# 951 no-operations on TensorE, 45 regroupings and 9 loads on ScalarE's queue, and another order, in a cross attention with layer normalisation

## The chip, the cores and the metric

The kernel runs on one core of one Trainium2 chip. The engines of a core are TensorE (PE; its weight loads are listed as PEld), VectorE (DVE), ScalarE (ACT), GpSimd (POOL) and SyncE (SP). SP computes nothing here; it issues DMAs, and ACT and POOL can issue them too, from the same stream that holds their computing instructions. The metric is the time of one execution in microseconds on the device. Before the change it is 519.78 us, the median of 3 runs (518.49 to 520.38).

## The reference, cut to what matters

```python
def ref(q, k, v, wq, wk, wv, wo, gamma, beta, mask):      # q: (4, 2048, 512), k = v: (4, 77, 512)
    qs = (q @ wq) in 16 heads of 32; ks_, vs = k @ wk, v @ wv in 16 heads of 32
    scores = einsum('bhqd,bhkd->bhqk', qs, ks_) / sqrt(32)
    scores = where(mask, -inf, scores)
    attn = einsum('bhqk,bhkd->bhqd', softmax(scores), vs)  # back to (4, 2048, 512)
    out = attn @ wo + q
    return (out - mean(out)) / sqrt(var(out) + 1e-5) * gamma + beta
```

8192 rows of queries, 77 keys in each of 4 batches, everything in float32. A float32 product of the two large projections is made as three products of rounded parts (high by high, low by high, high by low).

## The kernel before, in words

The 8192 rows are 64 tiles of 128; two tiles are a block, four a group. Each word of a long table, ORDER, is one step: a letter and the number of a group, tile or block. The program reads the table from left to right and each engine gets its instructions in that order; nothing else schedules. A second table, SLOTS, says which buffer each tile takes. Semaphore waits are added where one engine needs what another made, and where a buffer is overwritten.

- `g` loads a half group of the transposed x (xtf, line 262), `i` casts it to its high part (xth, ACT), `j` makes the low part (xtl, POOL). `Q` is a visit of TensorE to one of a group's four query projections: 12 matmuls of 128x512 into one bank (pq, line 275); `q` copies it out (DVE).
- `S` makes the scores of one tile: 32 matmuls in the program, which the chip runs as 64 with a weight load each (sc, line 405). `T` adds the mask and takes the maxima, a quarter of the heads at a time (DVE, line 422), `e` is the exponentials with their sums (ACT, line 437), `r` the reciprocals (DVE), `n` the normalising (POOL, line 452), `t` transposes 32x32 pieces of the tile into the block's buffer B (DVE, line 473).
- `P` with block, part and queue is one regrouping DMA (line 484): a block takes 12 of them, B to PT, which puts the keys on the partitions. The last block has `U`, the same by tile. The last letter names the issuing queue: s for SP, a for ACT, g for POOL. B and PT have two buffers each.
- `V` is the product with the values, 16 heads of one block (pa, line 498), `a` and `b` split it into a high part AH (ACT) and a low part AL (DVE), `O` is a visit to the output projection of one tile, 12 matmuls (po, line 554). `x` loads the residual rows (line 539), `+` adds them (DVE), `s` takes the moments, `v` the reciprocal square root (POOL), `k` scales (ACT), `f` and `)` apply gamma and beta (POOL), `w` stores (SP, line 601).

A queue handles its steps in order: a regrouping on SP that waits for its transposition holds the loads and stores behind it, and one on ACT or POOL holds that engine's computing instructions behind it. A block's `V` comes three blocks after its scores, so each engine works on other tiles at one time. Where the values' product follows a score tile, `early_waits` puts the product's DMA waits ahead of that tile.

Of the kernel before, what the change touches and what calls it, by code (L numbers as in the profile page):

```python
# [8 lines left out]
F32 = mybir.dt.float32  # L9
# [4 lines left out]
ALU = mybir.AluOpType  # L14
# [3 lines left out]
P = 128  # L18
# [16 lines left out]
for b in range(4):  # L35
# [15 lines left out]
T1.1 Q4 T1.2 e0.3 F0 T1.3 I0 e1.2 r0 n0 S2 q4 e1.0 S3 T2.3 T2.0 Q7 N Y0 x1 Q5 i5 F1 e1.1 F3 R2 e1.3 j5 i4 t0 T2.2 r1  # L51
F2 n1 e2.2 g6 T3.3 T3.0 T3.2 T2.1 j4 t1 P0.3s P0.2s P0.0s P0.5s e3.3 Q6 q6 G0 q7 B0 B2 e2.0 G3 G1 D0 e2.1 q5 e3.2 T3.1
P0.9s e2.3 r2 e3.1 e3.0 i6 G2 g7 P0.10s P0.11s S4 T4.3 e4.3 P0.7s T4.2 P0.8s i7 e4.2 B1 r3 Z1.s T4.0 e4.0 n2 T4.1 t2
Z0.s Q10 P0.4s n3 t3 P0.6s D2 P0.1s Z3.s S6 T6.2 T6.0 j6 D1 T6.3 P1.3s q10 T6.1 e4.1 r4 P1.0s P1.5s Q9 q9 e6.0 S5 T5.2
T5.0 e6.1 P1.2s P1.1s P1.8s j7 Q14 Z16.s P1.6s n4 t4 S7 Z2.s T7.3 e5.2 e6.3 e6.2 e7.3 T7.0 e7.0 T7.2 T5.3 T5.1 r6
P1.11s T7.1 e7.1 e7.2 q14 P1.10s P1.9s P1.7s P1.4s Q8 q8 Q11 q11 r7 Q13 n6 t6 e5.3 e5.1 e5.0 S9 T9.0 n7 T9.3 t7 r5 n5
V1 a1.0 T9.1 T9.2 a1.1 e9.0 b1.1 b1.0 t5 Z11.s x3 g8 g9 Z5.s Z13.s V0 a0.0 a0.1 P3.9s P3.3s Q12 S8 q13 T8.0 T8.2 e9.1
P3.4s P3.5s e9.3 b0.0 T8.3 O3 S10 i8 b0.1 L1 e8.0 T10.0 x5 P2.9s +3 e9.2 P3.2s P2.3s r9 O2 T8.1 q12 P3.8s e8.3 j8
P2.5s x2 Z4.s P3.1s O1 P2.4s P3.7s s3 O0 P3.6s =24.8 T10.1 +2 P3.10s e8.2 e8.1 P3.0s P3.11s s2 Z12.s x0 T10.3 n9 Q15
r8 v1 e10.1 i9 P2.6s e10.3 g11 +1 P2.1s T10.2 P2.0s n8 P2.10s Y1 e10.0 t9 P2.11s +0 e10.2 k3 t8 Z6.s q15 S11 k2 j9  # L60
T11.2 T11.1 r10 x7 V3 S12 T11.0 Q17 Z15.s T12.1 P4.2s T11.3 s0 =16.8 s1 P4.4s i11 Q18 n10 Q16 e11.1 q17 a3.0 a3.1
P2.8s P2.7s T12.3 b3.1 f3 T12.2 )3 T12.0 e11.0 v0 P2.2s Z14.s b3.0 e11.2 t10 e11.3 P4.7s P4.6s S13 g10 q18 P4.9s j11
# [7 lines left out]
T18.2 b5.0 n16 +8 +9 T18.3 P6.1s t16 Q22 S19 V6 e17.3 q23 q22 P7.3s f5 P7.11s P7.7s x11 T19.1 P7.2s e17.1 T19.0 T19.2  # L70
r17 P7.0s i15 P7.5s e18.3 n17 w1 s9 a6.0 i14 e18.0 P7.9s P7.4s S20 O10 b6.0 j15 t17 a6.1 T19.3 s8 P7.6s T20.2 Q24
e18.2 Q27 r18 )4 T20.1 T20.3 x10 e19.2 e19.0 e19.3 e19.1 )6 +10 T20.0 S21 b6.1 P7.10s n18 )5 q27 q24 O12 e20.3 P7.8s
w4 g16 O11 s10 P8.11s e20.1 w6 e20.2 r19 n19 e20.0 x12 P8.9s t18 T21.1 T21.2 V7 v4 e21.2 j14 f7 T21.3 t19 P8.10s +12
S22 T21.0 r20 O13 P8.8s P8.6s P8.0s k8 )7 e21.1 k9 T22.1 Q26 T22.3 +11 a7.0 P8.2s P8.4s P8.1s T22.0 Q25 P9.9s P9.10s
# [21 lines left out]
n34 e36.0 e36.1 e35.0 P16.11s s27 )23 P16.2s O28 O29 P16.10s T36.3 t34 S37 P16.5s T36.2 +28 s28 f24 +29 r35 P16.7s
P16.0s e36.3 T37.1 T37.3 V15 j22 x32 n35 T37.2 w25 e36.2 g25 e37.1 e37.2 a15.1 S38 T37.0 a15.0 j23 t35 P17.9s r36
P17.2s n36 s29 T38.3 e37.0 s26 b15.0 T38.0 P17.5s Q42 T38.1 e37.3 P16.3s b15.1 Q41 Q43 q41 P16.8s v14 q42 T38.2 Q40
S39 )24 v13 t36 q43 q40 e38.3 k28 e38.0 r37 T39.3 x30 g24 V16 P17.4s e38.1 T39.2 e38.2 =56.8 k27 r38 P17.7s T39.1 n37
w23 P17.8s T39.0 t37 S40 P17.10s P17.3s i24 a16.0 a16.1 T40.0 i25 e39.1 T40.1 e39.2 P17.6s O30 j24 e39.3 n38 e39.0 k26  # L100
f27 T40.2 P17.1s j25 b16.0 f28 O31 b16.1 x31 P17.11s P17.0s O32 +30 s30 T40.3 e40.0 t38 g26 e40.1 e40.3 r39 S41 w24
P18.1s e40.2 +32 P18.2s +31 P18.9s n39 )28 T41.3 P18.4s P18.11s V17 T41.1 S42 k29 e41.3 T41.0 t39 r40 Q44 T42.3 Q45
)27 T42.2 P18.7s P18.8s e41.1 n40 f29 T42.1 a17.1 P18.6s P18.5s x33 O33 T41.2 q44 T42.0 P19.11s a17.0 P18.3s P19.0s
b17.0 b17.1 s31 e41.0 Q46 P18.0s P19.10s P19.4s P19.1s e42.2 w27 P18.10s P19.9s P19.7s e41.2 v15 e42.0 q45 r41 +33 )29
e42.3 V18 P19.3s s32 e42.1 s33 x34 t40 P19.5s q46 r42 a18.1 S43 Q47 k30 n41 w29 g27 T43.3 v16 k33 a18.0 e43.3 P19.8s
t41 i27 k31 T43.2 O34 P19.2s P19.6s T43.1 T43.0 b18.0 q47 f30 f33 S44 e43.1 n42 j27 f31 )31 t42 O35 w28 T44.3 T44.2
T44.1 P20.6s P20.9s f26 e43.0 +34 e43.2 P20.3s k32 S45 T44.0 V19 x35 P20.10s g28 i26 b18.1 O37 r43 n43 e44.3 )33 T45.1
# [67 lines left out]
def xattn_layernorm(  # L175
# [625 lines left out]
```

## Time and profile before

| what | us |
|---|---|
| median of 3 runs | 519.78 |
| the profiled execution | 521.82 |
| its span, first to last instruction | 519.9 |
| PE busy | 502.0 (97%) |
| ACT busy | 474.9 (91%) |
| DVE busy | 459.8 (88%) |
| POOL busy | 420.6 (81%) |
| mean granted clock of TensorE | 0.995 |

Busy time counts an engine as busy while an instruction of its own is in it. TensorE's matmuls overlap each other in the records (one is listed with 0.39 us and the next starts 0.23 later), so its busy share says little about holes; a timeline shows them in brackets, with what ended them. "issue" is said where the engine waited for nothing that the profile shows. SPq, ACTq and DVEq are the sequencers of those engines, which issue DMAs and handle waits. By kind, the DMAs before the change are 396 regroupings (344 issued by SP, 21 by ACT, 31 by POOL), 64 loads of residual rows, 64 stores and the loads of the transposed x, of weights and masks.

### The profile page before, as it was taken

How to read it: one execution, taken by the hardware profiler on the slowest of the kernel's cores; microseconds unless marked ns; L12 is line 12 of the kernel's file. 1: busy time of each engine (PE TensorE's matmuls, PEld its weight loads, DVE VectorE, ACT ScalarE, POOL GpSimd, SP SyncE). 2: the span in 40 equal slices, each digit the busy share in tenths (PEclk: the TensorE clock that was granted, in tenths of full speed). 3: DMA queues.
4: the chain of work that ended last, by engine and by line, in shares of the span. 5: the costliest groups of instructions: out<-in, count | busy, mean ns of one | idle time of the engine just before them, and what ended most of it. 6: DMA issues, size and time to landing. Idle time of an engine off the chain costs nothing.

```text
span 519.9 us, 20339 instructions
## 1 busy us (share of the span) xinstructions
PE 502.0 (97%) x6831; PEld 386.9 (74%) x6831; DVE 459.8 (88%) x2539; ACT 474.9 (91%) x2248; POOL 420.6 (81%) x387
## 2 busy tenths in 40 slices
PE   9999999999999998999999999999999998999895
PEld 7987778776677776777687777778777776877664
DVE  6799998998979897899898999897989988999987
ACT  6699999998999998799989999999998798899872
POOL 3566447886858999698789979799998989899986
PEclk9999999999999998999999999999999999999999
DMA  8947667889867786688877797867795859878657
GB/s 309 395 173 174 146 178 191 217 211 212 249 179 194 186 258 174 193 223 240 223 217 195 200 244 195 233 196 201 225 264 153 240 163 224 229 216 214 170 156 270
DMA packets 58782, 110.86 MB, mean 213 GB/s; under 512 B 9462, under 2 KB 11278, under 8 KB 58678
## 3 DMA queue, kind: packets, MB, share of 16 engines
q1 hardware_dynamic: 54502, 101.30, 69.0%
q0 software_dynamic: 2496, 5.77, 4.1%
q10 hardware_dynamic: 1680, 2.49, 1.9%
q8 instruction: 54, 0.88, 0.8%
q14 instruction: 50, 0.41, 0.3%
HBM read 41.79 MB, written 16.78 MB: 113 GB/s over the span
## 4 chain that ended last, share of the span: by engine, by line
PE 62%; POOL 10%; ACT 7%; DMA 7%; SPq 5%; DVE 4%; issue 3%; DVEq 0%; ACTq 0%; POOLq 0%
PE pq L275 25%; PE po L554 19%; PE sc L405 8%; PE pa L498 7%; ACT pbuf L437 5%; POOL pbuf L452 4%; DMA PT<-B 4%; SPq L484 3%; DVE B L473 2%; POOL o L598 2%; PE pv L326 2%; POOL PT L484 1%; PE pk L299 1%; PE pq L685 1%; ACT o L592 1%
## 5 line engine op out<-in xcount | busy, mean ns | idle before, releaser
L437 ACT ACTIVATE pbuf<-pbuf,nm 128x77 f32<-128x77 f32 x1024 | 352.3, 350 | 13.2 <-DVE nm L422 9.0
L437 ACT ACTIVATION_READ_ACCUMULATOR pbuf<-pbuf,nm 128x1 f32 x1024 | 195.0, 190 | 0.0
L452 POOL TENSOR_TENSOR pbuf<-pbuf,ri 128x1232 f32<-128x1232 f32 x63 | 142.3, 2259 | 50.6 <-DVE ri L447 37.3
L422 DVE CUSTOM_DVE_ANT_0 pbuf<-sc,mb 128x77 f32<-128x77 f32 x1024 | 170.2, 231 | 7.9 <-PE sc L405 5.4
L473 DVE STREAM_TRANSPOSE B<-pbuf 128x1280 f32<-128x1280 f32 x64 | 96.1, 1503 | 16.6 <-POOL pbuf L452 7.5
L554 PE MATMUL po<-woh,AH 128*128 128x512 f32 x256 | 103.8, 405 | 0.0
L554 PE MATMUL po<-wol,AH 128*128 128x512 f32 x256 | 100.6, 393 | 0.0
L554 PE MATMUL po<-woh,AL 128*128 128x512 f32 x256 | 100.5, 393 | 0.0
L275 PE MATMUL pq<-xth,wqh 128*128 128x512 f32 (+1 forms) x256 | 99.9, 390 | 0.2
L275 PE MATMUL pq<-xtl,wqh 128*128 128x512 f32 (+1 forms) x256 | 98.2, 383 | 0.0
L275 PE MATMUL pq<-xth,wql 128*128 128x512 f32 (+1 forms) x256 | 98.1, 383 | 0.0
L422 DVE DVE_READ_ACCUMULATOR2_ANT nm<- 128x1 f32 x1024 | 83.7, 82 | 0.0
L405 PEld LDWEIGHTS sc<-kct,q 32*64 32x64 f32 x4096 | 52.8, 130 | 31.9 <-issue 19.9
L595 POOL TENSOR_TENSOR o<-o,gam 128x512 f32<-128x512 f32 x56 | 72.0, 1291 | 2.3 <-ACT o L592 2.1
L598 POOL TENSOR_TENSOR o<-o,bet 128x512 f32<-128x512 f32 x56 | 71.8, 1290 | 1.1
L269 POOL TENSOR_TENSOR xtl<-xtf,xth 128x1024 fp32r<-128x1024 f32 x28 | 67.1, 2400 | 6.9 <-ACT xth L265 6.2
L405 PE MATMUL sc<-kct,q 32*64 32x77 f32 x4096 | 63.6, 238 | 7.7 <-issue 3.7
L498 PE MATMUL pa<-PT,vsb 96*32 96x256 f32 x992 | 59.8, 382 | 2.7 <-DMA xtl<-x 2.0
L554 PEld LDWEIGHTS po<-woh,AH 128*128 128x128 f32 x256 | 48.3, 189 | 14.3 <-issue 1.1
L275 PEld LDWEIGHTS pq<-xth,wqh 128*128 128x128 f32 x256 | 48.2, 188 | 11.4 <-issue 0.8
L554 PEld LDWEIGHTS po<-woh,AL 128*128 128x128 f32 x256 | 48.5, 189 | 10.6
L275 PEld LDWEIGHTS pq<-xth,wql 128*128 128x128 f32 x256 | 48.1, 188 | 9.6
(108 smaller groups left out, 638.7 us busy)
## 6 DMA issues: line engine op xcount, KB each, us to landing
PT<-B SPq DMA_DIRECT2D x330, 128.0 KB
xtf<-xT SPq DMA_DIRECT2D x28, 512.0 KB
o<-x SPq DMA_DIRECT2D x56, 256.0 KB
out<-o SPq DMA_DIRECT2D x56, 256.0 KB
PT<-B POOLq DMA_DIRECT2D x25, 128.0 KB, 4.6
PT<-B ACTq DMA_DIRECT2D x17, 128.0 KB
stage_a<-kin SPq DMA_DIRECT2D x4, 410.0 KB
xtf<-xT SPq DMA_DIRECT2D x4, 256.0 KB
```

Of the source, the lines that this page charges most:

```text
L269: return nc.gpsimd.tensor_tensor(l[:, c : c + 2], fx.pop((g, c)), xh[g][:, c : c + 2].bitcast(F32), ALU.subtract)
L275: nc.tensor.matmul(pq, w[:, c, m * P : (m + 1) * P], r[g][:, c, rs], start=(n == 0), stop=(n == 11))
L405: mm = nc.tensor.matmul(sc[j][r0 : r0 + SR, g * NK : (g + 1) * NK], qs[q, g, rs.start + r0 : rs.start + r0 + SR], kct[q, g, t // TPB, keys ...
L422: nc.vector.tensor_tensor_reduce(pb[:, h // 2, (h % 2) * NK : (h % 2 + 1) * NK], scs[t][j][:, g * NK : (g + 1) * NK], mb[:, t % TPB, keys_ ...
L437: nc.scalar.activation(pb[:, h // 2, (h % 2) * NK : (h % 2 + 1) * NK], pb[:, h // 2, (h % 2) * NK : (h % 2 + 1) * NK], AF.Exp, bias=nmax[t ...
L452: return nc.gpsimd.tensor_tensor(pv, pv, rv.to_broadcast((P, NP, 2, NK)), ALU.mult)
L473: nc.vector.transpose(bt.rearrange("p c q r -> p q c r"), pbuf[t % NPB].rearrange("p q (c r) -> p q c r", c=5),)
L484: parts.setdefault(b, []).append(queue.dma_start(pt[32 * c : 32 * c + 32, i, :, cols], src))
L498: nc.tensor.matmul(pas[b, g // 2][HD * j : HD * (j + 1), (g % 2) * BLK : (g % 2 + 1) * BLK], vsb[:, 2 * b // TPB, h % 2, HD * (h // 2) : H ...
L554: nc.tensor.matmul(pos[t], a[:, c, rs], w[:, c, :], start=(first and c == 0 and n == 0), stop=(c == NC_D - 1 and n == 2),)
L595: return nc.gpsimd.tensor_tensor(od[t], od[t], gam, ALU.mult)
L598: return nc.gpsimd.tensor_tensor(od[t], od[t], bet, ALU.add)
```

## The change: what it does

Every step of ORDER is still there once, so each engine computes the same operations with the same shapes. Four things differ.

1. `Q` and `O` may carry a number after a dot: so many no-operations are spread among the 12 matmuls of the visit, at most 24, two behind each matmul. 951 are in the program, in visits from group 1's query projection (Q4.16) to group 14's, and one in the output projection of tile 57.
2. The queue letters of 82 regroupings differ. 39 go from SP to ACT, 14 from ACT to SP, 21 from POOL to SP, 5 from SP to POOL and 3 from POOL to ACT. ACT then issues 49 (45 for blocks and 4 for the last block's tiles), POOL 12, SP 335. Before, ACT's and POOL's stood in blocks 23 to 31; now ACT's stand in most blocks from 3 on.
3. `x` may carry a 1: ACT issues that load. These are the loads of tiles 13, 14, 27, 46, 52, 56, 58, 60 and 63. (`g` and `q` have such a switch too, which no word uses, and so has `k`, so the sets CENTRED and IN_PSUM are empty.)
4. The order of the words differs from the 200th word on, and with it some buffers in SLOTS.

```diff
-T1.1 Q4 T1.2 e0.3 F0 T1.3 I0 e1.2 r0 n0 S2 q4 e1.0 S3 T2.3 T2.0 Q7 N Y0 x1 Q5 i5 F1 e1.1 F3 R2 e1.3 j5 i4 t0 T2.2 r1
+T1.1 Q4.16 T1.2 e0.3 F0 T1.3 I0 e1.2 r0 n0 S2 q4 e1.0 S3 T2.3 T2.0 Q7.24 N Y0 x1 Q5.21 i5 F1 e1.1 F3 R2 e1.3 j5 i4 t0
...
-    def q_rows(pq, m, g, rs):
+    def pad(n, nops):
+        for _ in range((n + 1) * nops // 12 - n * nops // 12):
+            nc.tensor.nop(hint="pad")
+
+    def q_rows(pq, m, g, rs, nops=0):
...
                 nc.tensor.matmul(pq, w[:, c, m * P : (m + 1) * P], r[g][:, c, rs], start=(n == 0), stop=(n == 11))
+                pad(n, nops)
                 n += 1
...
-    def load_x(t):
+    def load_x(t, by_scalar):
...
-        nc.sync.dma_start(od[t], x[t * P : (t + 1) * P, :])
+        (nc.scalar if by_scalar else nc.sync).dma_start(od[t], x[t * P : (t + 1) * P, :])
...
-    def o_proj(t):
+    def o_proj(t, nops=0):
...
                     stop=(c == NC_D - 1 and n == 2),
                 )
+                pad(3 * c + n, nops)
...
-        "Q": lambda k, part: q_visit(*divmod(k, 4)), "q": lambda k, part: q_evac(*divmod(k, 4)),
+        "Q": lambda k, part: q_visit(*divmod(k, 4), part), "q": lambda k, part: q_evac(*divmod(k, 4), part),
...
-        "x": lambda k, part: load_x(k), "X": lambda k, part: resid(k), "O": lambda k, part: o_proj(k),
+        "x": lambda k, part: load_x(k, part), "X": lambda k, part: resid(k), "O": lambda k, part: o_proj(k, part),
```

TensorE behind the scores of tile 26, the place of the longest hole in its timeline before. Names carry a number of their own at the end; sc is a bank of scores, po one of the output projection. Before:

```order
1585 L405 MATMUL sc_2_3557<-kct,q_2919 64x77
1586 L405 MATMUL sc_3_3558<-kct,q_2919 64x77
1587 L554 MATMUL po_3614<-woh,AH_3374 128x512
1588 L554 MATMUL po_3614<-wol,AH_3374 128x512
1589 L554 MATMUL po_3614<-woh,AL_3394 128x512
```

and now:

```order
1811 L414 MATMUL sc_2_3948<-kct,q_3220 64x77
1812 L414 MATMUL sc_3_3949<-kct,q_3220 64x77
1813 L563 MATMUL po_4013<-woh,AH_3653 128x512
1814 L276 NO_OP x2
1815 L563 MATMUL po_4013<-wol,AH_3653 128x512
1816 L276 NO_OP x2
1817 L563 MATMUL po_4013<-woh,AL_3749 128x512
1818 L276 NO_OP x2
```

The output projection that follows these scores carries 24 no-operations, and 226 rows more stand ahead of it than before.

SP's queue at the regroupings of blocks 13 and 14 before (PT_14 is block 14's; o_22 a load of residual rows):

```order
176 L262 DMA xtf_10_0_4376<-xT 128x1024
177 L484 DMA PT_14_4380<-B_14_4327 32x2x512 x2
178 L484 DMA PT_13_4169<-B_13_3991 32x2x512
179 L539 DMA o_22_4394<-x 128x512
180 L484 DMA PT_13_4169<-B_13_3991 32x2x512
181 L484 DMA PT_14_4380<-B_14_4327 32x2x512
182 L539 DMA o_23_4434<-x 128x512
183 L484 DMA PT_13_4169<-B_13_3991 32x2x512 x2
184 L484 DMA PT_14_4380<-B_14_4327 32x2x512 x2
```

Now three of block 14's are on ACT, between exponentials, scalings of o and casts of AH:

```order
186 L536 CAST AH_12_4925<-pa_12_0_4854 128x512
187 L493 DMA PT_14_4954<-B_14_4820 32x2x512
188 L609 ACTIVATE o_21_4573<-o_21_4573,rn_10_4877 128x512
189 L609 ACTIVATE o_19_4334<-o_19_4334,rn_9_4822 128x512
190 L536 CAST AH_12_4925<-pa_12_1_4855 128x512
191 L446 ACTIVATE pbuf1_81,sum_31_4846<-pbuf1_81,nm_31_4827 128x77 x8
192 L493 DMA PT_14_4954<-B_14_4820 32x2x512
```

POOL behind the normalising of tile 53 before, with regroupings of block 26 among its products with gamma and beta:

```order
285 L452 TENSOR_TENSOR pbuf2_82<-pbuf2_82,ri_53_7530 128x8x154
286 L595 TENSOR_TENSOR o_44_7263<-o_44_7263,gam_76 128x512
287 L484 DMA PT_26_7702<-B_26_7528 32x2x512 x3
288 L595 TENSOR_TENSOR o_45_7341<-o_45_7341,gam_76 128x512
289 L598 TENSOR_TENSOR o_44_7263<-o_44_7263,bet_77 128x512
290 L484 DMA PT_26_7702<-B_26_7528 32x2x512
291 L452 TENSOR_TENSOR pbuf0_80<-pbuf0_80,ri_54_7704 128x8x154
```

and now, without them:

```order
285 L461 TENSOR_TENSOR pbuf2_82<-pbuf2_82,ri_53_8503 128x8x154
286 L272 TENSOR_TENSOR xtl_15_8357<-xtf_15_2_7888,xth_15_8161 128x1024
287 L612 TENSOR_TENSOR o_45_8086<-o_45_8086,gam_76 128x512
288 L612 TENSOR_TENSOR o_44_8224<-o_44_8224,gam_76 128x512
289 L615 TENSOR_TENSOR o_45_8086<-o_45_8086,bet_77 128x512
290 L461 TENSOR_TENSOR pbuf0_80<-pbuf0_80,ri_54_8696 128x8x154
```

Block 26 had seven regroupings on POOL and ACT; now it has two, on ACT.

More of the change, by code (lines that the diff above doesn't have):

```diff
@@ L70 @@
[L70 to L74, printed above, removed]
@@ L96 @@
[L96 to L100, printed above, removed]
@@ L101 @@
[L101 to L105, printed above, removed]
@@ new lines @@
+T42.1 T42.2 k31 Q45.8 i24 Q46 P19.4s e42.3 q45 P19.3s q47 T42.0 r40 a17.1 e42.1 e42.0 v16 =48.8 q44 V18 b17.1 n41 g26
+)26 n40 f31 t41 a18.0 P19.7a P19.9s t40 q46 S43 T43.1 w29 k32 P19.11s b18.0 O34 T43.0 +34 T43.2 a18.1 T43.3 k30 P20.0s
+O35.11 P20.10a e42.2 r42 x35 P20.7s S44 T44.1 j24 b18.1 T44.3 f32 )31 P20.11s T44.0 P19.8s f27 P19.10a Q48.24 +35
+T44.2 e43.1 e43.2 )27 w31 P19.1s n42 )32 i26 P19.5s w27 e43.0 t42 S45 O36.24 x36 P20.2s g27 k33 s34 e44.3 x37 e43.3
+T45.2 Q51.24 w26 P20.3a V19 j26 q48 f30 e44.1 T45.3 r43 e44.2 P20.6a P20.4s P20.8s P20.1s +36 g29 T45.0 P20.5s e44.0
@@ new lines @@
+n43 f33 q51 i27 e45.3 P20.9s )33 a19.0 e45.0 w32 s36 T45.1 )30 t43 P21.10s s35 P21.11a e45.1 r44 S46 a19.1 P21.8g
+T46.1 e45.2 n44 e46.1 x40 O37.17 P21.1s v17 b19.0 +37 T46.2 j27 P21.5s T46.3 T46.0 Q50 P21.2s Q49.24 P21.9s P21.7s r45
+e46.2 e46.0 t44 k34 b19.1 n45 S47 q50 q49 k35 f35 T47.1 V20 T47.2 P21.3s e46.3 T47.0 s37 P21.0s v18 i29 g28 f34 e47.0
+t45 S48 a20.0 O39.24 k36 T48.2 b20.0 T48.0 w30 )34 x39 w33 r46 +39 T47.3 T48.3 P22.6s x38 a20.1 e47.2 k37 O38.22 Q55.2
+i28 n46 T48.1 b20.1 P21.4s P22.2s +38 S49 O40.13 =56.8 e47.1 f36 w34 f37 e47.3 x42 P21.6s s38 e48.0 O41.15 e48.2
@@ L142 @@
+U63.3g b30.1 ~57 U62.0s U63.6g U63.8g y56 k54 u56 &58 O61 O60 y59 s58 U62.8a W62 y57 f55 k53 u58 U63.2s &61 u57 ~61
+)55 U63.0s w52 z56 w48 z59 c62 y58 &60 w51 z57 W63 y61 X63 d62 w59 w55 w56 z58 u61 ~60 f53 c63 z61 w49 w61 y60 d63 O62
+w57 u60 f54 )54 )53 z60 w54 w60 w58 w53 &62 s62 u62 O63 y62 s63 z62 y63 u63 w62 z63 w63
 """
 ALONE = {int(w[1:]) for w in ORDER.split() if w[0] in "u@"}
+CENTRED = {int(w[1:].split(".")[0]) for w in ORDER.split() if w[0] == "k" and "." in w}
+IN_PSUM = {int(w[1:].split(".")[0]) for w in ORDER.split() if w[0] == "k" and w.endswith(".2")}
@@ L739, in xattn_layernorm @@
             ins = ops[op](int(k or 0), int(part or 0))
-            if op in "FG":
+            if op in "FG" or op == "k" and k and int(k) in CENTRED - IN_PSUM:
                 shared = ins
-            elif shared and op in "jnf)":
-                wait_for(ins, shared, "VectorE's pass over two tiles of SBUF is begun ahead of GpSimd's")
+            elif shared and op in "jnf)v":
+                wait_for(ins, shared, "VectorE's pass over both of its ports is begun ahead of GpSimd's")
                 shared = None
```

207 lines of the change are left out of this document (109 added, 98 removed).

## The prediction

> **What bounds the kernel now.** I read the page's busy line first, then the chain of waits in order of time, then TensorE's timeline where that chain leaves it, and last the queues' own waits.
>
> ```profile
> PE 502.0 (97%) x6831; PEld 386.9 (74%) x6831; DVE 459.8 (88%) x2539; ACT 474.9 (91%) x2248; POOL 420.6 (81%) x387
> 126.41 2.72 PE po L554 x12
> 132.73 1.86 PE pa L498 x32
> 139.83 2.97 PE po L554 x12
> 148.23 0.88 PE sc L405 x52
> ```
>
> The rows of the chain are start, length, what. TensorE's visits have fixed lengths: a projection visit (pq or po, 12 matmuls) 2.72 us, or 2.97 between two visits of another shape; a score tile (sc) 0.88, a values product (pa) 1.86. With 64 po, 60 pq, 64 sc and 32 pa visits that is 174 + 163 + 56 + 60 = 453 us of a span of 519.9, and the rest is the start (the first 21 us), the changes of shape and the holes. So TensorE sets the time wherever it is not waiting, and what can be won is the sum of its holes. The timeline of TensorE shows them in brackets:
>
> ```profile
> 119.03 0.94 PE L405 MATMUL sc<-kct,q 32*64 32x77 f32 x64 [0.85 <-DMA PT<-B]
> 122.53 0.73 PE L405 MATMUL sc<-kct,q 32*64 32x77 f32 x40 [0.23 <-DVE nm L422]
> 138.81 1.02 PE L405 MATMUL sc<-kct,q 32*64 32x77 f32 x60 [0.97 <-issue]
> 151.99 0.35 PE L405 MATMUL sc<-kct,q 32*64 32x77 f32 x4 [0.16 <-issue]
> 199.53 0.29 PE L405 MATMUL sc<-kct,q 32*64 32x77 f32 x2 [2.59 <-issue]
> 254.60 1.05 PE L405 MATMUL sc<-kct,q 32*64 32x77 f32 x64 [0.39 <-DMA out<-o]
> 258.12 0.31 PE L405 MATMUL sc<-kct,q 32*64 32x77 f32 x2 [0.33 <-DVE nm L422]
> 258.75 0.89 PE L405 MATMUL sc<-kct,q 32*64 32x77 f32 x58 [0.32 <-DVE nm L422]
> 438.60 0.94 PE L405 MATMUL sc<-kct,q 32*64 32x77 f32 x64 [1.53 <-DMA PT<-B]
> 442.08 0.89 PE L405 MATMUL sc<-kct,q 32*64 32x77 f32 x58 [0.32 <-DVE nm L422]
> 482.09 1.93 PE L498 MATMUL pa<-PT,vsb 96*32 96x256 f32 x32 [0.78 <-DMA out<-o]
> 494.41 1.94 PE L498 MATMUL pa<-PT,vsb 96*32 96x256 f32 x32 [1.97 <-DMA xtl<-x]
> 507.01 1.08 PE L513 MATMUL pa<-PT,vsb 96*32 96x128 f32 x32 [0.21 <-DMA out<-o]
> ```
>
> Three holes have the releaser "issue" and stand in the middle of a score tile: 0.97 + 0.16 + 2.59 = 3.72 us. Seven follow a regrouping or VectorE's maxima: 0.85 + 0.23 + 0.39 + 0.33 + 0.32 + 1.53 + 0.32 = 3.97. Three are in the last 40 us: 0.78 + 1.97 + 0.21 = 2.96. Together 10.65 us.
>
> **The no-operations (the "issue" holes).** No tile is late at these three holes, so the instruction itself was. The page's queue list and a count between the holes say why:
>
> ```profile
> q8 instruction: 54, 0.88, 0.8%
> 138.83:151.99 13.16, 13.00 (x253) 10.02 (x252) 11.47 (x68) 13.16 (x63) 5.98 (x5) 1.00 0.80 236
> 151.99:199.53 47.54, 44.95 (x626) 34.40 (x627) 41.39 (x234) 47.54 (x237) 44.16 (x36) 1.00 0.70 193
> ```
>
> The stage rows count TensorE's matmuls and weight loads: 253 + 252 between the first two holes, 626 + 627 between the second and the third. With the 9 and 27 semaphore waits that the built program has there (and an edge of one or two), this is 512 and 1280, that is 2 and 5 times 256; and 54 instruction packets for 13,662 matmuls and loads are one for each 253. TensorE's instructions come in blocks of 256, and each of these holes is the first instruction of a block. Counted on from there, the shortest block of the kernel before (a score tile, a values product, most of a second score tile) is consumed in 3.2 us, and the hole at 199.53 shows a block that came later than its use. In the changed order, counting each no-operation as one instruction, I summed by the visit lengths above the work between a block's predecessor's start and its own, with the issue allowed half a score tile (64 instructions) of lead, an assumption: the smallest such time is 3.6 us before and 7.1 us after, and 2 blocks were under 4 us before, none after. So 951 no-operations move the block edges out of the dense stretches. The last hole costs more than itself:
>
> ```profile
> 196.94 2.59 issue
> 199.82 4.54 PE po L554 x12
> 200.00:250.00 50.00, 50.00 (x643) 38.70 (x643) 45.22 (x258) 44.91 (x212) 42.49 (x39) 0.97 0.78 217
> ```
>
> The visit behind it took 4.54 instead of 2.97, with a granted clock of 0.97 in that stage: 1.6 us. All of it is 3.72 + 1.6 = 5.3 us; bounds 0 and -5.3. I take **-4.7**, nearly all, since every margin at least doubles where it was tight. The Trainium skill (Runtime: NRT & Kernel Launch, Instruction fetch mechanics) gives blocks of 256 instructions, as the count does, but calls the crossing "mostly hidden"; the trace has 2.59 us for one, so the trace decides; by the page this term would be 0 and the sum 4.7 us higher.
>
> Their own price: the trace has no no-operation, so I go to the nearest rows, instructions that only the sequencer handles.
>
> ```profile
> 254.26 0.05 DVEq L473
> 254.31 0.05 issue
> 254.36 0.05 DVEq L473
> ```
>
> One wait and the gap behind it are 0.10 us. A visit carries at most 24 no-operations, 2.4 us; its 24 loads and matmuls are issued at no more than 0.88 / 128 = 0.007 us each (a score tile issues 128), 0.17 us. 2.57 is under the 2.72 for which the array is busy, so that visit hides them. If the cover is gone, because a wait had emptied TensorE's queue, the following score tile starts without lead; the row at 138.81 shows 1.02 us for a tile that starts so, against 0.88. Bounds 0 and 25 such tiles at 0.14, +3.5; I take **+1.0**, nearer to 0, as such waits are few.
>
> **The regroupings and loads.** A block of two tiles is regrouped by 12 DMAs, 344 of the 396 issues on SP. The chain and the queue's waits:
>
> ```profile
> SPq L484 <- DVE B L473: 77.7, 25, 7.4
> 242.73 1.44 DVE B L473
> 250.40 1.24 SPq L484
> 251.68 2.54 DMA PT<-B
> 113.10 5.84 DMA PT<-B
> ```
>
> From the end of a transposition (242.73 + 1.44 = 244.17) to the issue that the next one waits for (250.40 + 1.24 = 251.64) pass 7.5 us in which SP issues one DMA after the other, regroupings of blocks 13 and 14 and x loads between them; the transfer itself takes 2.5. The next transposition must wait, since it overwrites the same B buffer, and behind it on VectorE stand maxima that the score tiles' banks wait for: the holes at 254.60 to 258.75. The one at 119.03 ends the same way behind a transfer of 5.84. The change puts 3 of block 14's regroupings and one of block 13's on ScalarE, one more of 13 on GpSimd, and x loads of tiles 13, 14, 27, 46, 52, 56, 58, 60 and 63 on ScalarE. Three issues fewer at 0.6 us are 1.9 us off that chain, more than any of these holes but the sum at 438 to 442 (1.85). Bounds 0 and -4.0; I take **-3.5**, since 39 regroupings leave SP for ScalarE in blocks 3 to 30. The Trainium skill (DMA: Bandwidth & Descriptors, Issuing engines are not separate DMA queues) says issuing from several engines saves only the sequencer's time, "usually small relative to the DMA itself". Here 7.5 us of issue stand against 2.5 of transfer, so the trace disagrees; by the page this term would be near 0.
>
> From block 23 on the other direction rules: GpSimd issues 12 regroupings in all instead of 31, and 14 of ScalarE's go to SP.
>
> ```profile
> L484 POOL DMA_DIRECT2D PT<-B x31 | 17.3, 562 | 3.8 <-issue 1.3 <-DVE nm L422 1.0 <-DMA out<-o 0.7
> 350.00:480.00 130.00, 128.15 (x1831) 98.27 (x1833) 117.01 (x670) 119.98 (x586) 119.39 (x121) 1.00 0.77 211
> ```
>
> 19 at 0.56 are 10.7 us given back to GpSimd, which is busy for 119.39 of 130 us there and carries the normalising that the last blocks wait for; SP had room. The tail's three holes (2.96) shrink by what GpSimd no longer issues ahead of the last products, 1 to 2 issues: **-1.0**, bounds +1 and -3.
>
> What ScalarE pays: 58 issues instead of 21, 37 more. Two rows of it:
>
> ```profile
> 408.29 0.59 ACTq L484 DMA_DIRECT2D PT<-B  x1
> 408.93 0.36 ACT L437 ACTIVATE pbuf<-pbuf,nm 128x77 f32<-128x77 f32 x1 [2.71 <-DVE nm L422]
> 409.15 0.59 ACTq L484 DMA_DIRECT2D PT<-B  x1
> 409.20 0.19 ACT L437 ACTIVATION_READ_ACCUMULATOR pbuf<-pbuf,nm 128x1 f32 x1
> 100.00:350.00 250.00, 244.17 (x3427) 187.17 (x3426) 223.56 (x1299) 241.27 (x1155) 212.71 (x176) 0.99 0.78 212
> ```
>
> The second issue lies under exponentials that were already queued and costs nothing; the first came into an idle engine and, if that idle had ended sooner, would cost 0.59. If all 37 were bare it is 22 us of ScalarE, which has 250 - 241.27 = 8.7 us of idle in the middle stretch; if all are covered, 0. The new ones stand among runs of exponentials, like the second. What waits behind one, at block 14: two scalings, the cast of AH of block 12 and then exponentials. I take **+0.9**: a few bare ones, mostly in ScalarE's own idle time.
>
> **The order.** Engines' operations are the same in number and shape. TensorE enters and leaves its projections 47 and 46 times instead of 49 and 48; a pair of such changes is 2.97 - 2.72 = 0.25: **-0.5**.
>
> **Sum.** -4.7 + 1.0 - 3.5 - 1.0 + 0.9 - 0.5 = -7.8. The profiled execution took 521.82 us (span 519.9 and 1.9 around it), so 514.0 by its own measure; the median of the runs shown, 519.78, is 2.04 below it, so **512.0** against that median.
>
> **Rivals.** (1) The block edges fall elsewhere than I count, or the blocks come late through the load on the DMA engines (0.70 to 0.80 share in the rows above) whatever the margin: then only the no-operations' price stays of that part, -7.8 + 4.7 = -3.1, 516.7. For it speaks the hole at 138.81, whose block is not among the shortest; against it, all three holes stand exactly on the edges. Its chance is 0.18. (2) The holes only move: ScalarE (91%) and VectorE (88%) have little more room than TensorE, and a tile that is scored sooner waits for its exponentials; 519.8, chance 0.12. (3) Slower: an issue on ScalarE waits for a transposition and all exponentials stand behind it. SP waited for one in 25 of its regroupings, 77.7 us, 3.1 each, 7% of 344. If ScalarE meets the same at its 49 regroupings, 49 x 0.07 x 3.1 = 11 us are lost, more than -7.8 wins: 523. It decides from some 10 us of such waits on. Against it: before, the ScalarE group of exponentials waits only 1.8 us in all for a regrouping:
>
> ```profile
> L437 ACT ACTIVATE pbuf<-pbuf,nm 128x77 f32<-128x77 f32 x1024 | 352.3, 350 | 13.2 <-DVE nm L422 9.0 <-DMA PT<-B 1.8 <-POOL pbuf L464 1.2
> ```
>
> Chance 0.10.
>
> **How the numbers follow.** The forecast has 0.60, the rivals 0.18, 0.12 and 0.10. Faster by over 0.5% means below 517.2, slower above 522.4; half a per cent is what a measurement of this kernel can tell from no change. The forecast nearly always and three quarters of rival 1 are faster: 0.59 + 0.14 = 0.73. Same: the rest of these and most of rival 2, 0.17; slower 0.10. All holes of TensorE gone (10.65) with the slow visit (1.6) and the changes of shape (0.5) give 521.82 - 12.75 - 2.04 = 507.0; the waits also stretch visits that show no hole, some 3 us (the visit before 119.03 among them), so the low end is 504.0. The high end, 519.5, takes in rival 1 and the nearer half of rival 2.
>
> **What would show it.** Right: no hole of "issue" inside a score tile, no stage with a clock under 1.00 before the tail, 57 or 58 instruction packets on q8, SP's wait for B well under 77.7, and score tiles at 0.88 behind padded visits. Wrong: score tiles of 1.0 us and more behind padded visits (the no-operations are not hidden), "issue" holes as before (rival 1), exponentials that wait for a transposition with a ScalarE issue ahead of them (rival 3), or the same 10 us of holes at other places (rival 2).

## The result, and the profile after

| | before | changed |
|---|---|---|
| median, us | 519.71 (516.25 to 525.76, 20 runs) | 516.66 (512.36 to 525.17, 20 runs) |
| ratio | | 0.9936, 95% interval 0.9911 to 0.9961 |

The change makes the kernel faster by 0.64%, some 3.3 us. That is the direction that was forecast and inside its range, but 7.8 us were expected: less than half came. The timed executions of one kernel spread over 9 us and more here, so small differences are read from the ratios and their intervals, and a single profile shows where a wait is and not how much time it is worth. The ratios leave out executions that took over 1.5% more than the fastest of their kernel; by the two medians alone it would be 0.9941. The profile of the changed kernel shown here is from a second run of the same code (ratio 0.9946, see the first experiment); its profiled execution took 515.81 us, its span 514.0. The execution profiled first took 521.18 us.

The busy line of the changed kernel, and its queue of instruction packets:

```profile
PE 500.9 (97%) x6831; PEld 385.9 (75%) x6831; DVE 457.7 (89%) x2539; ACT 474.0 (92%) x2248; POOL 410.8 (80%) x368
q8 instruction: 58, 0.95, 0.8%
```

TensorE still sets the time, with the same busy time less 1.1 us. The 58 packets are those of a program that is longer by 951 instructions. TensorE's timeline, all holes over 0.15 us behind the start (in brackets the hole and what ended it):

```profile
135.24 0.47 PE L282 MATMUL pq<-xth,wql 128*128 128x512 f32 x1 [0.59 <-issue]
250.97 0.90 PE L414 MATMUL sc<-kct,q 32*64 32x77 f32 x58 [0.23 <-DVE nm L431]
298.99 0.56 PE L414 MATMUL sc<-kct,q 32*64 32x77 f32 x34 [0.50 <-issue]
358.08 1.07 PE L507 MATMUL pa<-PT,vsb 96*32 96x256 f32 x16 [0.71 <-DVE AL L540]
360.00 0.31 PE L414 MATMUL sc<-kct,q 32*64 32x77 f32 x2 [0.38 <-DVE nm L431]
360.64 0.89 PE L414 MATMUL sc<-kct,q 32*64 32x77 f32 x58 [0.32 <-DVE nm L431]
406.38 0.31 PE L414 MATMUL sc<-kct,q 32*64 32x77 f32 x2 [0.38 <-DVE nm L431]
406.92 0.90 PE L414 MATMUL sc<-kct,q 32*64 32x77 f32 x58 [0.23 <-DVE nm L431]
437.36 0.89 PE L414 MATMUL sc<-kct,q 32*64 32x77 f32 x58 [0.32 <-DVE nm L431]
452.76 0.34 PE L414 MATMUL sc<-kct,q 32*64 32x77 f32 x2 [0.16 <-DVE q L298]
453.38 0.90 PE L414 MATMUL sc<-kct,q 32*64 32x77 f32 x58 [0.28 <-DVE nm L431]
477.56 1.93 PE L507 MATMUL pa<-PT,vsb 96*32 96x256 f32 x32 [0.95 <-DVE o L575]
```

Together they are 5.05 us where the kernel before had 10.65. "issue" is 1.09 of it (3.72 before), and no hole is longer than 0.95 (2.59 before). No hole ends with a regrouping here; those that end with VectorE's maxima (nm) remain, at other places.

The execution profiled first is less clean. Its holes over 0.15 us are 8.07 us in all, one of them behind a regrouping (0.37), and its two of "issue" are 2.48:

```profile
135.88 0.47 PE L282 MATMUL pq<-xth,wql 128*128 128x512 f32 x1 [1.61 <-issue]
442.59 0.52 PE L414 MATMUL sc<-kct,q 32*64 32x77 f32 x30 [0.87 <-issue]
```

So the signs that the prediction named came in part: 58 packets and score tiles at 0.88 came, but each profile has a hole of "issue" inside a score tile, and the first one has a stage (from 250 us) at a clock of 0.97.

### The profile page after: what moved, and what is told of

It reads as the page before. It is cut to its first block, busy times and chain, and to the rows that moved or that the text cites. A ratio compares the mean times of both kernels' runs of the same rounds, so it can differ in the third digit from the quotient of the medians.

```text
span 519.4 us, 21286 instructions
## 1 busy us (share of the span) xinstructions
PE 503.4 (97%) x6831; PEld 387.5 (75%) x6831; DVE 459.0 (88%) x2539; ACT 474.6 (91%) x2248; POOL 411.2 (79%) x368
## 4 chain that ended last, share of the span: by engine, by line
PE 48%; POOL 12%; DMA 11%; ACT 9%; DVE 9%; SPq 5%; issue 5%; ACTq 0%; DVEq 0%; POOLq 0%
PE pq L282 18%; PE po L563 16%; ACT pbuf L446 7%; PE sc L414 6%; PE pa L507 5%; DMA PT<-B 5%; SPq L493 4%; POOL pbuf L461 4%; DVE pbuf L431 3%; POOL o L615 2%; DVE B L482 2%; POOL xtl L272 2%; DMA o<-x 2%; POOL o L612 2%; DMA out<-o 2%
## 5 line engine op out<-in xcount | busy, mean ns | idle before, releaser
L446 ACT ACTIVATE pbuf<-pbuf,nm 128x77 f32<-128x77 f32 x1024 | 355.9, 383 | 15.3 <-DMA o<-x 6.1
L446 ACT ACTIVATION_READ_ACCUMULATOR pbuf<-pbuf,nm 128x1 f32 x1024 | 228.8, 223 | 0.0
L414 PEld LDWEIGHTS sc<-kct,q 32*64 32x64 f32 x4096 | 54.0, 130 | 29.9 <-issue 14.9
L414 PE MATMUL sc<-kct,q 32*64 32x77 f32 x4096 | 65.6, 238 | 4.7 <-DVE nm L431 3.2
L563 PEld LDWEIGHTS po<-woh,AL 128*128 128x128 f32 x256 | 48.1, 188 | 10.5
```

The source lines that it names most:

```text
L414: mm = nc.tensor.matmul(sc[j][r0 : r0 + SR, g * NK : (g + 1) * NK], qs[q, g, rs.start + r0 : rs.start + r0 + SR], kct[q, g, t // TPB, keys ...
L446: nc.scalar.activation(pb[:, h // 2, (h % 2) * NK : (h % 2 + 1) * NK], pb[:, h // 2, (h % 2) * NK : (h % 2 + 1) * NK], AF.Exp, bias=nmax[t ...
L563: nc.tensor.matmul(pos[t], a[:, c, rs], w[:, c, :], start=(first and c == 0 and n == 0), stop=(c == NC_D - 1 and n == 2),)
```

## The experiments

In all of them "changed" is the changed kernel and "before" the kernel before; every ratio is against the kernel before, timed on the same chip. One per cent is 5.2 us.

### The parts, taken away from the changed kernel

**The same code again** (no edit).

> The changed kernel once more, timed against the kernel before on one chip, so that the other runs of this set have it beside them. Expected 0.9936 of before within 0.3%, some 516.5 us. Theory A (the no-operations removed most of the instruction holes, and the moved regroupings only moved the other holes): the profile again has at most one or two holes of issue, and waits for VectorE's maxima at several score tiles that together are 8 to 13 us of stretched visits. Theory B (all parts gave a little): holes of both kinds are shorter than before.

0.9946 [0.9908, 0.9984], median 516.63.

**Without the no-operations:**

```diff
-Q4.16 ... Q7.24 ... Q5.21 ...
+Q4 ... Q7 ... Q5 ...          (all 951 taken away)
```

> The changed order, queues and loads, without the 951 no-operations. Edges of blocks of 256 instructions fall again where they fall; five blocks hold less than 5 us of TensorE's work counted from 33 instructions ahead of the block before, against none with the no-operations. Theory A: 2 to 5 us longer than the changed kernel, near 520, with 2 to 5 holes of issue inside score tiles, some with a visit at a lower clock behind them. Rival (the no-operations neither help nor cost): within 1 us of the changed kernel, 516.5. Rival (they cost sequencer time): 1 to 3 us shorter, 514.

1.0012 [0.9974, 1.0050], median 521.87. TensorE's waits of this kernel (us in total, times, longest):

```profile
PE sc L414 <- issue: 3.5, 2, 2.4
PE pa L507 <- DMA PT<-B: 2.7, 1, 2.7
PE pa L507 <- DVE AL L540: 1.9, 1, 1.9
```

and of the changed kernel, those of "issue":

```profile
PE pq L282 <- issue: 0.6, 1, 0.6
PE sc L414 <- issue: 0.5, 1, 0.5
```

The no-operations are worth 1.0012 - 0.9946 = 0.66%, 3.4 us (the two intervals, taken together, leave 0.6 to 6.2), and without them the kernel is as fast as the one before. Everything else in the change is thus worth +0.6 us, between -1.4 and +2.6, where the forecast had -4.1.

**All block edges moved by 61 instructions**, by leaving 61 of the 951 out near the start:

```diff
-Q4.16 ... Q7.24 ... Q5.21
+Q4 ... Q7 ... Q5
```

> The changed kernel with the first three padded visits (Q4, Q7, Q5 of group 1) bare: 61 no-operations fewer, 890 left at the same places. Every later edge of a block of 256 moves by 61 instructions, into the dense stretches: 9 blocks then hold less than 5 us of work, 6 of them 3.4. Theory A (what counts is where the edges fall): longer than the kernel without any no-operations or equal to it, 520 to 525, with 4 or more holes of issue. Rival (what counts is that no-operations slow TensorE's issue): within 1 us of the changed kernel, 516.5.

1.0243 [1.0194, 1.0292], median 533.1: 3% slower than the changed kernel, with 890 of its 951 no-operations and the same work in the same order, and slower than the 520 to 525 us that were expected. Its waits and its chain at the first hole:

```profile
PE sc L414 <- issue: 8.8, 6, 2.4
PE po L563 <- issue: 2.1, 1, 2.1
```

```profile
94.85 2.42 issue
97.79 11.20 PE pq L282 x36
```

The changed kernel's chain at the same three projection visits:

```profile
95.24 8.40 PE pq L282 x36
```

Three visits take 11.20 us behind the hole and 8.40 without it: the hole of 2.42 costs 2.8 more in the visits that follow. The granted clock says why: it is 0.50 behind that hole (columns as in the stage rows of the prediction):

```profile
97.50:100.00 2.50, 2.50 (x9) 1.88 (x8) 2.16 (x27) 2.50 (x15) 2.27 (x1) 0.50 0.89 252
```

The stage from 300 to 350 us, with a hole of 2.32, has a clock of 0.93, and that is 3.5 us of 50. Over the timed executions the median granted clock is 0.994 in the changed kernel, 0.988 without the no-operations and 0.979 shifted. By estimate, these are 3.1 and 7.7 of 514 us. In the shifted kernel the holes of "issue" (10.9 us against 1.1) and the clock together are about what the shift costs, 16.5 us. What the 3.4 us of the no-operations are made of is less clear: in the profile without them the clock falls behind three holes, and only one of these is of "issue" (2.36); the others wait for VectorE (1.85) and for a regrouping (2.67). The Trainium skill (TensorE: Matmul & The Clock Gate, Part 1: The HAM clock gate) has the gate close after an idle window of about 3.4 us. These traces differ: the clock was 0.50 behind holes of 1.85 and 2.42 us, and 1.00 behind one of 2.13 in the shifted kernel and one of 3.32 in the kernel with the old queues. So the length of the hole alone doesn't decide.

**The issuing queues as before**, order and no-operations as changed:

```diff
-P3.5a ... P2.0g ... x13.1
+P3.5s ... P2.0s ... x13       (82 regroupings and 9 loads)
```

> The changed order and its no-operations, but every regrouping on the queue that it had before, and all loads of residual rows on SP. Theory A: within 1.5 us of the changed kernel (516.5), since its regroupings still left 8 to 13 us of waits. The term as I put it before: 4.5 us longer (regroupings and tail, less what ScalarE pays), 520 to 521. Rival (ScalarE's issues cost more than they give): 1 to 4 us shorter, 513 to 515.

1.0126 [1.0079, 1.0173], median 525.89. The queues are worth 1.8%, 9.4 us, in the changed order: almost three times the 3.5 us that the prediction gave them, and more than any of the three expectations.

**Only the order**, without no-operations and with the queues as before.

> The changed order alone: no no-operations, every regrouping and load on the queue that it had before. With the two single undoings known (no-operations 0.66%, queues 1.8%), parts that add up give 0.9946 x 1.0066 x 1.018 = 1.019 of before, some 530. Theory C (the new order was found together with its queues and edges and is worse without them: the order term is +9 us, not -0.5): 1.015 to 1.025, 527 to 533. Theory D (the parts overlap, the order by itself is neutral as I priced it): within 0.4% of before, 518 to 522.

1.0233 [1.0186, 1.0281], median 533.22. The order, which the prediction priced at -0.5 us, costs 12.1 us when nothing else goes with it. With the no-operations (the kernel above) it costs 6.6, so in this order they are worth 1.1% with the old queues and 0.7% with the new ones.

### The parts, put into the kernel before

**The new queues in the order before** (the same 82 letters and 9 loads):

> The order of before, without no-operations, with the changed kernel's queue for every regrouping and its nine loads on ScalarE. Theory C (queues are worth their 9 us only in the order they were found with): within 0.5% of before or slower, 518 to 524. Theory D (the queues are worth this in any order): 508 to 513. My term for them was -3.5 - 1.0 + 0.9 = -3.6: 516.

1.0155 [1.0120, 1.0189], median 526.85: 8.1 us slower. The letters that win 9.4 us in one order lose 8.1 in the other.

**Block edges out of the dense stretches, in the order before.** 829 no-operations were spread so that no block of 256 holds less than 6.4 us of TensorE's work, by the visit lengths of the prediction and with 33 instructions of lead:

```diff
-Q5 ... Q6 ... Q9
+Q5.9 ... Q6.1 ... Q9.15       (and others, 829 in all)
```

> The order and queues of before, with 829 no-operations in other visits, chosen so that no block of 256 instructions holds less than 6.4 us of TensorE's work, counted from 33 instructions ahead of the block before (6 of the blocks before the change hold less than 5). Theory A (edges alone): 3 to 5 us faster than before, 515 to 517, no or one hole of issue. Rival (no-operations help only with the changed order): within 1 us of before.

1.0094 [1.0059, 1.0130], median 524.75. The holes of "issue" fell to one, of 2.0 us, but the regroupings that come last cost more at the same places, as its waits show:

```profile
PE sc L413 <- DMA PT<-B: 4.0, 2, 2.7
PE pa L506 <- DMA PT<-B: 2.9, 1, 2.9
```

Before, the first of these was 0.85 + 1.53. In the second profile of the kernel before they were 0.88 + 1.34, and a values' product there waited 1.8 for one. So edges alone, chosen without the order, were no gain; this was expected to win and lost 4.9 us. Why it lost so much isn't shown.

**Both** (new queues and those 829 no-operations in the order before):

> The order of before with these 829 no-operations and the changed kernel's queues and loads. Theory D (both transfer): 505 to 509, which would beat both kernels. Theory C (only the edges transfer): 514 to 520, as with the edges alone or a little worse.

1.0158 [1.0131, 1.0186], median 527.3. On top of the new queues (1.0155) these no-operations change nothing.

### Which issues

The queue letters in two halves, blocks up to 22 with the loads of tiles 13, 14, 27, and blocks from 23 on with the other six loads; each half put into the order before, and each taken back in the changed kernel.

> The order before, with the changed kernel's issuing queues only for the regroupings up to block 22 (33 from SP to ScalarE, 4 from SP to GpSimd) and for the loads of x of tiles 13, 14 and 27. If the regrouping term of the prediction was a gain that goes over to any order: -3.5 us, ratio 0.993, and the holes behind 119.0, 122.5 and 254.6 to 258.8 shrink. If a queue is worth only what its own order makes of it: slower or the same, ratio 1.000 to 1.010 (up to the 1.0155 that all queues cost in this order), and the holes move to other places.

> The order before, with the changed kernel's issuing queues only from block 23 on (21 regroupings from GpSimd to SP, 14 from ScalarE to SP, 6 from SP to ScalarE, 3 from GpSimd to ScalarE, 1 from SP to GpSimd) and for the loads of tiles 46, 52, 56, 58, 60, 63. If the relief of GpSimd is a gain that goes over: -1.0 us, ratio 0.998. If SP, which gets 35 regroupings there at some 0.6 us of issue each, becomes the late one: +0.7 to +1.5%, ratio 1.007 to 1.015, with SP's wait ahead of PT<-B in the holes behind 350 us. The two halves add to the 1.0155 of both together if the cost is local to a place.

> The changed kernel, with the issuing queues of before for regroupings up to block 22 and for the loads of tiles 13, 14, 27. If the early part of the regrouping term stands as predicted: +3.5 us, ratio 1.007 against the changed kernel (1.000 against the kernel before). If these letters cost or win nothing by themselves: as the changed kernel, 0.994 to 0.995 against the kernel before.

> The changed kernel, with the issuing queues of before from block 23 on and for the loads of tiles 46, 52, 56, 58, 60, 63. If the late part is worth what the prediction gave it: +1.0 us, 0.996 against the kernel before. If the 1.8% that all old queues cost in the changed order lie here (the waits at the output projections of tiles 22 and 52 were one early and one late): up to 1.010 against the kernel before.

| new letters | order before | changed order |
|---|---|---|
| none | 1 | 1.0126 [1.0079, 1.0173] |
| up to block 22 | 1.0123 [1.0069, 1.0177] | 1.0095 [1.0062, 1.0127] |
| from block 23 on | 1.0046 [1.0006, 1.0086] | 1.0036 [0.9999, 1.0073] |
| all | 1.0155 [1.0120, 1.0189] | 0.9946 [0.9908, 0.9984] |

In the order before, each half costs, and the two together cost about their sum (1.69% against 1.55%). In the changed order the late half wins 0.9% alone and 1.5% on top of the early one; the early half wins 0.9% on top of the late one, and its 0.3% alone is inside the intervals. So the worth of a letter is made by the order around it.

Then only the 9 loads, or only ScalarE's 49 regroupings, were given back to SP in the changed kernel:

```diff
-x13.1 ...
+x13 ...                       (first of the two)
-P3.5a ...
+P3.5s ...                     (second of the two)
```

> The changed kernel, with the 9 loads of x back on SP. SP then issues 9 more DMAs at some 0.6 us, spread over the whole program. If the loads matter little: as the changed kernel, 0.994 against the kernel before. If they carry the worth of the queues: up to 1.012.

> The changed kernel, with ScalarE's 49 regroupings issued by SP, the loads left on ScalarE. If moving SP's issues is what the new order needs: 1.010 or more against the kernel before, and a wait of some 28 us in all ahead of the transpositions, as with the old queues, against 10.5 in the changed kernel. If ScalarE's own cost (idle of some 12 us that ends with one of its issues) outweighs it: 0.995 or less.

0.9938 [0.9902, 0.9973] and 1.0049 [1.0009, 1.0089]. The loads are worth nothing, the 49 regroupings 1.0%, 5.4 us. The first theory expected 1.010 or more for these and a wait of some 28 us ahead of the transpositions; it is 13.7, so this theory holds in part at most. The Trainium skill (DMA: Bandwidth & Descriptors, Issuing engines are not separate DMA queues) says that issuing from several engines saves only the issue time, usually small relative to the DMA. One issue is 0.6 us here against 2.5 for a transfer, which agrees; that 49 issues on another queue are worth 5.4 us is also a matter of what each had to stand behind, and the run doesn't separate the two. None of these kernels is faster than the changed one by more than the intervals; the one with its loads on SP is as fast.

### Where the order meets the queues

One group differs between most of these kernels: VectorE's transpositions into B (busy, mean ns, then the idle time ahead of them and what ended it). They wait for the normalised tile, and until the regroupings of two blocks earlier have left that buffer. Before:

```profile
L473 DVE STREAM_TRANSPOSE B<-pbuf 128x1280 f32<-128x1280 f32 x64 | 96.1, 1503 | 16.6 <-POOL pbuf L452 7.5 <-DMA out<-o 4.9 <-DMA PT<-B 3.4
```

The order alone:

```profile
L482 DVE STREAM_TRANSPOSE B<-pbuf 128x1280 f32<-128x1280 f32 x64 | 96.1, 1502 | 28.8 <-POOL pbuf L461 12.3 <-DMA out<-o 8.0 <-POOL rn L599 2.5
```

The changed kernel:

```profile
L482 DVE STREAM_TRANSPOSE B<-pbuf 128x1280 f32<-128x1280 f32 x64 | 96.1, 1503 | 10.5 <-POOL pbuf L461 4.5 <-DMA PT<-B 2.4 <-POOL o L612 1.7
```

Without the no-operations:

```profile
L482 DVE STREAM_TRANSPOSE B<-pbuf 128x1280 f32<-128x1280 f32 x64 | 96.1, 1502 | 8.5 <-POOL pbuf L461 2.8 <-DMA PT<-B 2.0 <-POOL rn L595 1.7
```

And the new queues in the order before:

```profile
L481 DVE STREAM_TRANSPOSE B<-pbuf 128x1280 f32<-128x1280 f32 x64 | 96.1, 1504 | 17.8 <-POOL pbuf L460 7.2 <-POOL o L611 4.4 <-DMA PT<-B 3.1
```

The new order with the old queues makes the transpositions wait 12 us longer than before, with or without no-operations (28.5 and 28.8); the new queues take 18 to 20 us of it away, and each half alone some 8 to 10 (19.0 with the late letters taken back, 20.6 with the early ones). In the order before, the same letters take nothing away (17.8 against 16.6, or 14.8 in a second profile). That answers to the signs of the table in the changed order. It doesn't answer to its sizes: without the no-operations the wait is 8 us shorter than before, and the time is the same; and 28.5 and 28.8 stand beside 1.0126 and 1.0233. And why the letters cost 8 us in the order before is only in part seen: exponentials there wait longer for a regrouping. Before, that was 1.8 us; with the new queues:

```profile
L445 ACT ACTIVATE pbuf<-pbuf,nm 128x77 f32<-128x77 f32 x1024 | 352.6, 352 | 16.4 <-DMA PT<-B 6.1 <-DVE nm L430 4.4 <-DMA out<-o 2.5
```

3.2 us more in all, and that is idle time of ScalarE, not shown to be time of the kernel. What makes up the 8.1 us stays open.

In the changed order TensorE's own holes show more. With the old queues it has two large ones:

```profile
249.48 0.78 PE L414 MATMUL sc<-kct,q 32*64 32x77 f32 x41 [3.32 <-DMA PT<-B]
474.95 0.50 PE L563 MATMUL po<-woh,AH 128*128 128x512 f32 x1 [2.96 <-DVE nm L431]
```

The changed kernel has neither. Together they are 6.3 us, beside the 9.4 that the old queues cost. The first comes back where early letters are taken back: 4.00 in the order alone, 3.26 with the early half taken back, 4.63 with only ScalarE's regroupings on SP. The second comes back with the old late letters: 3.01 in the order alone, 2.23 with the late half taken back. The chain to it in the kernel with the old queues starts at GpSimd:

```profile
468.64 1.03 POOL PT L493 x2
469.69 2.28 POOL pbuf L461
471.99 1.51 DVE B L482
474.95 8.50 PE po L563 x36
```

GpSimd issues five regroupings around there, 2.7 us, and behind them come the normalising, the transposition, the maxima and TensorE. In the changed kernel GpSimd issues none at that place. So in this order the relief of GpSimd works as the prediction described it, at a hole that neither profile of the order before has.

### The kernel before, once more

> The kernel before, once more. If the profiled execution on which the sum was made is typical: holes of TensorE behind 'issue' of some 3.7 us at the same three places, and a wait of some 16.6 us in all ahead of the transpositions into B. If the holes differ from one execution to the next: other places or less than half the size, and the sum rested on one sample.

1.0028 [0.9985, 1.0071], median 520.3, and a second profile (522.97 us). TensorE's holes in it, in part:

```profile
118.68 0.94 PE L405 MATMUL sc<-kct,q 32*64 32x77 f32 x64 [0.88 <-DMA PT<-B]
...
150.89 0.35 PE L405 MATMUL sc<-kct,q 32*64 32x77 f32 x4 [0.37 <-issue]
196.97 0.29 PE L405 MATMUL sc<-kct,q 32*64 32x77 f32 x2 [1.10 <-issue]
...
434.50 0.94 PE L405 MATMUL sc<-kct,q 32*64 32x77 f32 x64 [1.34 <-DMA PT<-B]
...
478.87 3.20 PE L498 MATMUL pa<-PT,vsb 96*32 96x256 f32 x32 [1.57 <-DVE B L473]
506.51 1.82 PE L513 MATMUL pa<-PT,vsb 96*32 96x128 f32 x32 [1.78 <-DMA PT<-B]
```

The holes that end with a regrouping at 119 and 434 came again with their size (0.85 and 1.53 in the first profile). Those of "issue" came at the same instructions (with 4 and 2 matmuls left of the same score tiles) but not with the same size: 1.10 for 2.59, 0.37 for 0.16, and the one of 0.97 doesn't show. Nor did the slow visit behind it come again. The rows of that stage and of the last one:

```profile
200.00:250.00 50.00, 49.19 (x646) 38.30 (x646) 44.75 (x259) 47.18 (x224) 44.35 (x40) 1.00 0.81 226
...
480.00:515.00 35.00, 33.04 (x214) 24.11 (x206) 26.54 (x74) 20.82 (x78) 27.18 (x39) 0.86 0.65 202
```

The stage from 200 us has the full clock, where the first profile had 0.97; this execution lost its time in the tail, at 0.86. So the 5.3 us of "issue" and of the slow visit were one draw: 1.5 us of it (of "issue") stood in the second.

## Why the prediction was right or wrong

| step | predicted, us | measured, us |
|---|---|---|
| no-operations, holes and price | -4.7 + 1.0 = -3.7 | -3.4 (-0.6 to -6.2) |
| queues, in the changed order (tail and ScalarE's price included) | -3.5 - 1.0 + 0.9 = -3.6 | -9.4 with the no-operations, -11.5 without (each within 3) |
| order, alone | -0.5 | +12.1 (+9.7 to +14.6) |
| order and queues together | -4.1 | +0.6 (-1.4 to +2.6) |
| sum | -7.8 | -3.3 (-2.0 to -4.6) |

**Right in the changed order: the no-operations move block edges.** The 58 packets and the sum of the term came; the shifted kernel shows that the position of the edges matters, since with nearly the same no-operations it loses 3% and has 10.9 us of "issue". The two profiles of the changed kernel have 1.09 and 2.48 us of "issue", those of the kernel before 3.72 and 1.47, so these profiles alone would not show the gain. Nor does it go over to the order before, from whose holes it was priced: the 829 no-operations cost 4.9 us there. Two sizes inside the term were off and offset each other, so that -3.4 came so near to -3.7 is luck. The holes of the kernel before were taken at their full 5.3 us from an execution that had more of them than the next one (1.5 us of "issue"), so -4.7 was too much. And the price of +1.0 doesn't show: score tiles behind padded visits take 0.88 as elsewhere. The changed kernel's chain, where the third visit of the first row and the whole of the second carry 24 no-operations each:

```profile
107.31 8.43 PE po L563 x36
115.73 2.72 PE pq L282 x12
118.45 0.88 PE sc L414 x54
```

**Wrong: the order at -0.5.** This is the step that failed. It was priced by the number of changes of shape on TensorE alone, on the argument that the operations are the same. The order also says when each transposition, regrouping and store comes, and with the old queues that costs 12.1 us. The prediction called the change four parts and added their prices, each worked out in the order before. But the parts had been fitted to each other: the queues win only in the changed order, and the changed order is worth something only with its queues. What was left of these two large terms, +12.1 and -11.5, was next to nothing. Taken in the other sequence, the new queues cost 8.1 and the order on top of them wins 7.4. Either way the two together are some 19.5 us better than the sum of their prices alone (+12.1 and +8.1 against +0.6), and the prediction had put this joint term at nothing without a reason. Why the new order is so bad with the old queues is seen for some 6 us (the two holes above); the rest stays open.

**Wrong in its size and in its ground: regroupings at -3.5 and the tail at -1.0.** The transposition's wait did fall, from 16.6 to 10.5, and SP's from 77.7 to 68.4 (71.8 in the execution profiled first), and holes that end with a regrouping are gone or small (0.37). But SP's wait is 82.9 with the same order and queues and no no-operations, so it doesn't follow the queues.

A shorter wait was taken for time one to one. It wasn't: the kernel without no-operations has a wait of 8.5 and is no faster than before. And the price was taken from the order before, where the same letters cost 8.1. The late letters with the relief of GpSimd (-1.0) were the other way in that order, too: +0.46%. The reading behind the term was off as well: the 7.5 us of issue that it set against one transfer of 2.5 are those of nine issues, and one is 0.6.

**Rival 3's mechanism exists and doesn't decide.** ScalarE does stop for a regrouping, with exponentials behind it, in the changed kernel:

```profile
343.41 0.19 ACT L446 ACTIVATION_READ_ACCUMULATOR pbuf<-pbuf,nm 128x1 f32 x1
346.02 0.59 ACTq L493 DMA_DIRECT2D PT<-B  x1
346.66 0.36 ACT L446 ACTIVATE pbuf<-pbuf,nm 128x77 f32<-128x77 f32 x1 [3.06 <-DMA PT<-B]
```

The idle time of exponentials that ends with a regrouping is 4.9 us in all (1.8 before), half of the 10 us from which this rival would decide, and ScalarE's idle ahead of its exponentials is about as long in all as before:

```profile
L446 ACT ACTIVATE pbuf<-pbuf,nm 128x77 f32<-128x77 f32 x1024 | 352.8, 352 | 11.5 <-DMA PT<-B 4.9
```

against 13.2; the other two profiles have 15.3 (changed) and 12.2 (before). **Rival 1** (the edges are late whatever the margin) is refuted by the shifted kernel, where the position of the edges makes 3%. Its time, 516.7, came, but by luck and for the opposite reason: that part of the sum held, and the rest fell. Something of it stands: the changed kernel keeps 1.1 to 2.5 us of "issue", where the prediction counted at least 7.1 us of work for every block. **Rival 2** (the holes only move) is right for order and queues: without the no-operations the holes over 0.15 us are 8.98 us in all, against 10.65 and 8.72 in the two profiles of the kernel before, at other places, and the time is the same.

## What to carry to other kernels

When a long order, its queues and its block edges were found together, price the parts only with each other: here the order alone cost 2.3%, the queues alone 1.6%, the edges alone 0.9%, and together they won 0.6%. A wait that shrinks on an engine beside the one that sets the time is not a gain until that engine's own holes shrink by as much. Before a hole goes into a sum, look at a second execution: those with a fixed place but a varying size are worth their mean.

## What the runs showed of the hardware

- No-operations between matmuls of 128x512, up to two behind each, don't lengthen the visit: one with 24 takes 2.72 us and the score tile behind it 0.88. That doesn't make them free in every kernel: 829 of them in the order before cost 0.9%, for a reason that isn't shown.
- The edge of a block of 256 instructions in a dense stretch costs up to 2.59 us (2.42 in the shifted kernel), and at times the clock as well: three visits of 11.20 instead of 8.40 us. Moving all edges by 61 instructions cost 3% of a kernel whose work was unchanged. The Trainium skill (Runtime: NRT & Kernel Launch, Instruction fetch mechanics) calls the crossing "mostly hidden". Most are here: the shifted kernel has 58 packets and seven holes of "issue". But these seven are 10.9 us. The size of one varies from one execution to the next: 2.59 and 1.10 us at the same instruction, 0.59 and 1.61 at another.
- The granted clock differs between kernels of the same work: the median over the executions is 0.994, 0.988 and 0.979 in the changed kernel, without its no-operations and with its edges shifted, and their times are 516.6, 521.9 and 533.1 us. Edges aren't all of it: with the edges kept and the old queues it is 0.987.
- After a hole on TensorE the granted clock was 0.50 for some us in some cases and 1.00 in others, whatever ended the hole: 0.50 behind 1.85 us (a wait for VectorE) and 2.42 ("issue"), 1.00 behind 2.13 ("issue") and 3.32 (a regrouping).
